# Two graph-attention layers: all source values made before the targets, adjacency masks transposed as pairs of bytes, and equal blocks of 1024 targets

## The chip, the core and the metric

The kernel runs on one core of one Trainium2 chip. The metric is the device time of one execution in microseconds (us). Before the change it is 3523.2 us, the median of three runs (3519.84 to 3524.52). The profiled execution has a span of 3524.0 us.

The engines are named as in the profile: PE is TensorE (PEld its weight loads), DVE is VectorE, ACT is ScalarE, POOL is GpSimd, SP is SyncE, whose queue issues the DMA transfers.

## What is computed

Three layers over 4096 nodes with 256 features, with one adjacency matrix `adj` (4096 x 4096, int32): two graph-attention layers and one masked transformer layer.

```python
def _gat_layer(x, adj_mat, W, a):              # 8 heads of O = 32
    Wh = einsum('nd,hdo->hno', x, W)
    src = einsum('hno,ho->hn', Wh, a[:, :O])
    dst = einsum('hno,ho->hn', Wh, a[:, O:])
    e = leaky_relu(src[:, :, None] + dst[:, None, :], 0.2)
    e = where(adj_mat[None] > 0, e, NEG_INF)
    alpha = softmax(e, axis=-1)
    return transpose(einsum('hnm,hmo->hno', alpha, Wh), (1, 0, 2)).reshape(N, -1)

h   = elu(_gat_layer(x, adj, W1, a1)) + x
out = elu(_gat_layer(h, adj, W2, a2)) + h
# then: layer norm, q/k/v, masked softmax attention, projection, feed-forward with gelu
```

The exponential of a leaky ReLU of a sum is one of two products of a factor of the target and a factor of the source; which one holds is a comparison of `src` with `-dst`. So a graph layer needs no exponential per pair: for each pair of nodes and each head it needs one bit, `src >= -dst` and `adj > 0`. These bits are made as bytes that TensorE reads as fp8, and the sums over the sources are matrix products of those bytes with tables of "values" (`vst`) of the sources. A last set of products with the mask alone gives the sum over all neighbours.

## The kernel before

A layer is a list of groups. A group is one block of targets, one pair of heads `p` and 512 sources `g` (four tiles `m` of 128). With eight target tiles it has 8 x 4 x 4 = 128 matmuls. "Chunk" stands below for 512 sources as they are prepared, `q` in the code.

```python
TILES = ((4, 4, 8, 8, 8), (8, 8, 8, 8))        # target tiles of 128, per layer and block

def mask_turn(w, k, t, r):                     # a unit of mask work: 128 targets, 1024 sources
    v = rows_p.tile([P, MC, P], BF, name="adj_bf", bufs=2)
    nc.vector.tensor_scalar(v..., r, 1.0, -(2.0**-30), op0=ALU.min, op1=ALU.max)   # the clip
    pt = turn_bank([P, MC, P], BF)             # two PSUM banks for all of this
    for m in range(MC):                        # MC = 8
        nc.tensor.transpose(pt[:, m, :], v[:, m, :], ident)
    nc.scalar.activation(staged[0]..., pt, AF.Identity, saturate=False)            # the eviction
    ...                                        # written to DRAM when 512 targets are done

def values(l, q, t):                           # the values of one tile of 128 sources
    pv = turn_bank([P, 512], F32)
    ...                                        # 2 matmuls, each issued as two passes
    nc.vector.tensor_scalar(L.negd[:, at, :], pv[...], -1.0, None, op0=ALU.mult)
    nc.scalar.activation(L.r[:, at, :], pv[...], AF.Exp, scale=LRELU - 1.0)        # g_r
    nc.vector.tensor_reduce(L.tops[...], pv[:, :D], AX.X, ALU.max, ...)            # g_tops
    for i in range(2):
        nc.scalar.activation(big[:, i, :], L.negd[:, at, :], AF.Exp, ...)
        nc.vector.tensor_scalar(prod[:, :, i, O], big[:, i, :], UP, None, op0=ALU.mult)
    nc.vector.tensor_tensor(prod[...], pv..., prod..., op=ALU.mult)                # the product
    nc.scalar.copy(halves[:, :, 0, :], part)                                       # the cast
    nc.vector.tensor_tensor(halves[:, :, 1, :], part, halves[:, :, 0, :], op=ALU.subtract)

def compare(l, nb, p, g, s_b):                 # the bytes of one group
    for i in range(G):                         # G = 4
        for j in range(2):
            if j == 1 or mt % MC == MC - 1:
                nc.scalar.activation(to.bitcast(I8), s, AF.Sign, bias=negd, scale=-1.0)   # L1021
            else:
                nc.vector.tensor_scalar(to, s, negd, None, op0=ALU.is_ge, saturate=False) # L1023
    nc.vector.tensor_tensor(both, both, mask..., op=ALU.bitwise_and)                      # L1026
```

At the start of a layer chunks 0 to 2 are prepared (`features`: transposes of the rows and two ACT copies; `term_rows`: a matmul, a copy and a store; four times `values`), then the groups begin, and chunks 3 to 7 are prepared in slots between the matmuls of the first groups. The comparisons of a group are made two groups ahead. After the last group of a pair of heads, `pair_end` works out its result on DVE and ACT in four steps that run beside later groups. The order on each engine is left to the scheduler of the programming framework.

The transformer follows: normalised rows and their q, k and v by matmuls (lines 1419 and 1440), the halves of q and k through DRAM into stacked tiles `u_k` and `u_q`, attention (lines 1480 to 1580) and projection with feed-forward (lines 1628 to 1676). There the first queries and masks are loaded after the last q/k/v block:

```python
        for nb in range(NNB):                  # q, k, v of 512 rows
            ...
            if i == 1:
                stack(k_st[:, :, cols], 1, (0, 0, 1, 1), cols)
        ...
        load_queries(0)
        for k in range(NT // MC):
            load_chunk(0, k)
        # attention follows, in an order fixed by the program
```

Of the kernel before, what the change touches and what calls it, by code (L numbers as in the profile page):

```python
# [14 lines left out]
U8 = mybir.dt.uint8  # L15
AF = mybir.ActivationFunctionType
# [5 lines left out]
P = 128  # L22
# [698 lines left out]
TILES = ((4, 4, 8, 8, 8), (8, 8, 8, 8))  # L721
# [27 lines left out]
def graph_attention(  # L749
# [32 lines left out]
    MC = 8  # L782
    G = 4
    NG = NT // G
# [9 lines left out]
    mask_p = ctx.enter_context(tc.tile_pool(name="g_mask", bufs=11))  # L794
    stage_p = ctx.enter_context(tc.tile_pool(name="g_stage", bufs=2))
    rows_p = ctx.enter_context(tc.tile_pool(name="g_rows", bufs=3))
# [8 lines left out]
    make_identity(nc, ident_f)  # L805

    vst = [keep.tile([P, G, H, 2 * VW], F16, name=f"vst{q}") for q in range(NG)]

    def turn_bank(shape, dtype):
        return ps.tile(shape, dtype, name="turn", tag="turn", bufs=2)  # L810

# [8 lines left out]
    nc.vector.tensor_scalar(checks.column(), pt[:, 0:1], 2.0**-20, None, op0=ALU.is_equal)  # L820


    masks = {}

    def mask_loads(w, k, t):

        r = rows_p.tile([P, MC * P], I32, name="g_rows")
        at = w * HB + t * P
        nc.sync.dma_start(r, adj[at : at + P, k * MC * P : (k + 1) * MC * P])
        return r  # L830

    staged = {}

    def mask_turn(w, k, t, r):

        if t == 0:
            if w == 0:
                staged[0] = mask_p.tile([P, 2, G, HB], F8, name="mask")
                views = [staged[0][:, i : i + 1] for i in range(2)]
                masks.setdefault((0, 0), []).extend(views)  # L840
            else:
                staged[0] = stage_p.tile([P, 2, G, HB], F8, name="stage")
        v = rows_p.tile([P, MC, P], BF, name="adj_bf", bufs=2)
        nc.vector.tensor_scalar(
            v.rearrange("p m s -> p (m s)"), r, 1.0, -(2.0**-30), op0=ALU.min, op1=ALU.max
        )
        pt = turn_bank([P, MC, P], BF)
        for m in range(MC):
            nc.tensor.transpose(pt[:, m, :], v[:, m, :], ident)  # L849
        nc.scalar.activation(  # L850
            staged[0].rearrange("p i g n -> p (i g) n")[:, :, t * P : (t + 1) * P],
            pt,
            AF.Identity,
            saturate=False,
        )
        if t == HB // P - 1:
            nc.sync.dma_start(
                mask_d[w][2 * k : 2 * k + 2].rearrange("c p n -> p c n"),
                staged[0].rearrange("p i g n -> p i (g n)").bitcast(U8),
            )  # L860

    def mask_fetch(l, nb, c):
        b = mask_p.tile([P, NW, G, HB], F8, name="mask")
        first = STARTS[l][nb] * P // HB
        n = TILES[l][nb] * P // HB
        for i in range(n):
            nc.sync.dma_start(
                b[:, i].rearrange("p g n -> p (g n)").bitcast(U8), mask_d[first + i][c]
            )
        masks.setdefault((l, nb), []).append(b[:, :n])  # L870
# [6 lines left out]
    for l, (w, a) in enumerate(weights):  # L877
        L = Layer()
        L.w_ext = keep.tile([P, DC, D + 2 * H], F32, name=f"g_w_ext{l}")
# [27 lines left out]
    def features(l, q):  # L907
# [5 lines left out]
        for c in range(DC):  # L913
            pt = turn_bank([P, HB], F32)
# [6 lines left out]
    def term_rows(l, q):  # L921

        L = layers[l]
        pr = turn_bank([P, HB], F32)
# [12 lines left out]
    def values(l, q, t):  # L937

        L = layers[l]
        pv = turn_bank([P, 512], F32)  # L940
# [31 lines left out]
        nc.vector.tensor_tensor(halves[:, :, 1, :], part, halves[:, :, 0, :], op=ALU.subtract)  # L972
# [9 lines left out]

    def preparation(l, q):

        steps = [lambda: (term_rows(l, q), values(l, q, 0))]
        steps += [lambda t=t: values(l, q, t) for t in range(1, G)]
        if q + 1 < NG:
            steps.insert(0, lambda: features(l, q + 1))
        else:
            steps.append(lambda: check_values(l))  # L990
        return steps
# [16 lines left out]
    def compare(l, nb, p, g, s_b):  # L1008

        L = layers[l]  # L1010
        nw = TILES[l][nb] * P // HB
        t8 = t_p.tile([P, 2, NW, G, HB], F8, name="t8")
        for i in range(G):
            mt = g * G + i
            for j in range(2):
                to = t8[:, j, :nw, i, :]
                s = s_b[:, j, : nw * HB].rearrange("p (w n) -> p w n", n=HB)
                negd = L.negd[:, mt, 2 * p + j : 2 * p + j + 1]

                if j == 1 or mt % MC == MC - 1:  # L1020
# [3 lines left out]
        both = t8[:, :, :nw].rearrange("p j w g n -> p j (w g n)").bitcast(I32)  # L1024
        mask = masks[l, nb][g].rearrange("p w g n -> p (w g n)").bitcast(I32)
        nc.vector.tensor_tensor(  # L1026
            both, both, mask.unsqueeze(1).to_broadcast(list(both.shape)), op=ALU.bitwise_and
        )
        return t8

    def pair_end(l, nb, p, ev):
# [37 lines left out]
        def step_divide():  # L1069
# [4 lines left out]
            z = block("e_z", O)  # L1074
            nc.vector.tensor_tensor(
                z, y[:, :, :, :O], inv.unsqueeze(3).to_broadcast([P, n, 2, O]), op=ALU.mult
# [5 lines left out]
        def step_out():  # L1082

            z, ex, x = (held[k].rearrange("p t j o -> p (t j o)") for k in ("z", "ex", "x"))
# [19 lines left out]

    turns = {}
    for nb in range(1, len(TILES[0])):
        first, n = STARTS[0][nb] * P // HB, TILES[0][nb] * P // HB
        units = [
            (first + i, k, t) for k in range(NT // MC) for i in range(n) for t in range(HB // P)
        ]  # L1110
        since, until = (NG, 3 * NG) if nb == 1 else (0, 3 * NG + 3)
        for u, unit in enumerate(units):
            at = (nb - 1) * per_block + since + u * (until - since) // len(units)
            turns.setdefault(at, []).append(unit)
    ordered = [u for i in sorted(turns) for u in turns[i]]
    loaded = {}
    AHEAD = 2

    def load_turns(n):

        while ordered and n > 0:
            u = ordered.pop(0)
            loaded[u] = mask_loads(*u)
            n -= 1
# [9 lines left out]
    def beside(i):  # L1134
# [5 lines left out]
        for u in turns.get(i, ()):  # L1140
            mask_turn(*u, loaded.pop(u))
            load_turns(1)
        if p + 1 == H // 2 and following(l, nb):
            for c in ((0, 1, 2), (), (), (3,), (4,), (5,), (6,), (7,))[g]:
                mask_fetch(*following(l, nb), c)

    def prepare(i):

        if i < len(groups):
            l, nb, p, g = groups[i]  # L1150
            s8[i] = compare(l, nb, p, g, s_of[l, nb, p])

    slots = []
    per = HB // P
    first_units = [(0, k, t) for k in range(NT // MC) for t in range(per)]
    ev = acc = None
    for i, (l, nb, p, g) in enumerate(groups):
        start = nb == 0 and p == 0
        if start and g == 0:

            features(l, 0)
            for q in range(2):
                for step in preparation(l, q):
                    step()
            while l > 0 and later:
                take()
            if l == 0:
                own = [mask_loads(*u) for u in first_units[:AHEAD]]
                for j in range(per):
# [591 lines left out]
```

## Time and profile before

| stage | from, us | to, us |
|---|---|---|
| graph layer 0 | 0 | 961 |
| graph layer 1 | 961 | 1783 |
| q, k, v | 1783 | 1893 |
| attention, with its start | 1893 | 3224 |
| projection and feed-forward | 3224 | 3524 |

The stages are read from the timeline: the last matmul of line 1234 of a layer, and the first and last of the lines named above.

| group of instructions | count | mean, ns |
|---|---|---|
| compare on ACT, 1024 targets (L1021) | 1008 | 1159 (1065 of busy time each, as they overlap) |
| compare on DVE, 1024 targets (L1023) | 784 | 746 (688 of busy time each) |
| AND with the mask, 2048 int32 (L1026) | 224 | 2288 |
| the same for half blocks, 1024 int32 | 64 | 1221 |
| clip (L844) | 128 | 685 |
| mask eviction (L850) | 128 | about 1035 |
| subtraction of `values` (L972) | 64 | 700 |

A window line of the profile gives the stretch, its length, then for PE, PEld, DVE, ACT and POOL the busy time with the number of instructions in brackets, then the granted TensorE clock (1.00 is full), the DMA share and GB/s. Restricted to one source line, it has only the engines of that line. A line of the list of groups gives line, engine, operation, output and inputs, shapes and count, then busy us and mean ns, then the idle time of the engine just before these instructions and what ended it. Of the 40 slices, each stands for 88 us, and a digit is the busy share in tenths.

### The profile page before, as it was taken

To read this page: it belongs to the slowest core of one execution; us is meant where nothing else is said; L and a number is where in the kernel's file an instruction comes from. 1 tells how busy PE (TensorE), PEld (TensorE's weight loads), DVE (VectorE), ACT (ScalarE), POOL (GpSimd) and SP (SyncE) were. 2 spreads that over 40 slices of the span, in tenths; PEclk is the share of its full clock that TensorE was granted. 3 is DMA by queue.
4 is the path that set the end of the run, shared out by engine and by line. 5 is a ranking of instruction groups with operands and counts; after the bars stand their busy time and mean duration, and the time that the engine had idled before them with its cause. 6 is when DMAs were issued, how large, how long until landed. Compare 5 with 4: busy or idle time off the path is not lost.

```text
span 3524.0 us, 99099 instructions
## 1 busy us (share of the span) xinstructions
PE 3357.4 (95%) x43715; PEld 2128.8 (60%) x43715; DVE 2903.2 (82%) x3580; ACT 2730.9 (77%) x3528; POOL 1239.1 (35%) x538
## 2 busy tenths in 40 slices
PE   6898999999989999999987999999999999997998
PEld 4698999999969999999963111111111121112666
DVE  5898999999889999999944999999999999996111
ACT  4799999998778888888854777777777777775332
POOL 0000000000000000000001999999999999996110
PEclk8999999999999999999998999999999999998999
DMA  4357554441221312111156010101010110002110
GB/s 140 123 191 242 167 167 157 157 123 39 68 62 33 86 39 80 45 58 37 26 135 171 10 40 13 37 19 31 25 25 25 25 37 13 28 9 68 44 47 25
DMA packets 199560, 252.76 MB, mean 72 GB/s; under 512 B 88080, under 2 KB 134672, under 8 KB 199120
## 3 DMA queue, kind: packets, MB, share of 16 engines
q1 hardware_dynamic: 199120, 246.34, 23.3%
q8 instruction: 344, 5.64, 0.7%
q14 instruction: 96, 0.79, 0.1%
HBM read 203.83 MB, written 42.47 MB: 70 GB/s over the span
## 4 chain that ended last, share of the span: by engine, by line
PE 73%; DVE 11%; ACT 9%; DMA 3%; issue 2%; POOL 2%; SPq 0%; DVEq 0%; ACTq 0%; POOLq 0%
PE bank L1234 34%; PE u_ps L1480 12%; PE u_av L1494 11%; PE u_dn L1494 6%; ACT t L1021 5%; DVE u_e L1489 4%; PE misc L1666 3%; PE misc L1419 2%; POOL u_both L1580 2%; DVE t L1023 1%; ACT u_ps L1487 1%; ACT stage L850 1%; DVE t L1026 1%; PE misc L1650 1%; PE turn L926 1%
## 5 line engine op out<-in xcount | busy, mean ns | idle before, releaser
L1234 PE MATMUL bank<-vst,t 128*128 128x66 f16 (+1 forms) x24576 | 1517.9, 203 | 22.0 <-DVE t L1026 15.5
L1234 PEld LDWEIGHTS <-t 128*128 128x128 fp8e4 x24576 | 1505.6, 97 | 33.2 <-DVE t L1026 18.0
L1234 PE MATMUL bank<-vst,mask 128*128 128x132 f16 x8192 | 1503.5, 222 | 0.0
L1021 ACT ACTIVATE t<-s_b,g_negd 128x1024 int8<-128x1024 f32 (+1 forms) x1296 | 1260.0, 1063 | 88.8 <-PE bank L1234 88.1
L1489 DVE SCALAR_TENSOR_TENSOR u_e<-u_mask,u_ps 128x1024 f32<-128x1024 uint8 x1024 | 1201.7, 1215 | 100.7 <-ACT u_ps L1487 95.8
L1580 POOL TENSOR_TENSOR u_both<-u_e 128x1024 f32<-128x1024 f32 x512 | 1199.8, 2367 | 238.5 <-DVE u_e L1489 238.3
L1487 ACT ACTIVATE u_ps<-u_ps 128x1024 f32<-128x1024 f32 x1024 | 1010.8, 1008 | 296.2 <-PE u_ps L1480 277.2
L1234 PEld LDWEIGHTS <-mask 128*128 128x128 fp8e4 x8192 | 803.6, 98 | 1.9 <-issue 0.9
L1026 DVE TENSOR_TENSOR t<-t,mask 128x2048 int32<-128x2048 int32 (+1 forms) x288 | 590.6, 2051 | 119.5 <-ACT t L1021 109.8
L1023 DVE TENSOR_SCALAR t<-s_b,g_negd 128x1024 fp8e4<-128x1024 f32 (+1 forms) x1008 | 638.5, 687 | 2.7 <-PE bank L1234 2.3
masks.py:197 POOL MEMSET u_ident<- 128x128 f32 x1 | 0.2, 204 | 1785.7 <-DMA u_wq<-in_L_gnn_w_qkv_dram 1785.7
L1480 PE MATMUL u_ps<-u_q,u_k 128*128 128x512 f16 x2048 | 580.5, 384 | 36.8 <-DMA u_q<-half_d 21.7
L1480 PEld LDWEIGHTS <-u_k 128*128 128x128 f16 x2048 | 139.2, 97 | 743.7 <-issue 685.4
L1494 PE MATMUL u_av<-u_e,u_v 128*32 128x512 f32 x4096 | 547.1, 605 | 0.0
L1494 PE MATMUL u_dn<-u_both,u_ones 128*32 128x512 f32 x2048 | 274.0, 605 | 1.3 <-POOL u_both L1580 1.3
L1494 PEld LDWEIGHTS u_av<-u_e,u_v 128*32 128x32 f32 x4096 | 80.9, 108 | 219.1 <-issue 211.3
L1657 ACT ACTIVATE u_hid<-misc,u_b 128x512 f32<-128x512 f32 x64 | 42.3, 683 | 142.9 <-PE misc L1650 142.8
L850 ACT ACTIVATE stage<-turn 128x1024 fp8e4<-128x1024 bf16 x112 | 114.2, 1037 | 1.1 <-PE turn L849 1.0
L1673 DVE TENSOR_TENSOR u_xres<-u_xres,misc 128x256 f32<-128x256 f32 x32 | 13.5, 421 | 122.7 <-PE misc L1666 122.7
L1666 PE MATMUL misc<-u_w,u_hid 128*128 128x256 f32 x512 | 111.8, 379 | 0.0
L1650 PE MATMUL misc<-ln_cols,u_w 128*128 128x512 f32 x256 | 111.2, 592 | 0.0
L1494 PEld LDWEIGHTS u_dn<-u_both,u_ones 128*32 128x32 f32 x2048 | 40.6, 108 | 110.9 <-issue 108.4
(104 smaller groups left out, 1749.8 us busy)
## 6 DMA issues: line engine op xcount, KB each, us to landing
g_rows<-in_adj_dram SPq DMA_DIRECT2D x128, 512.0 KB
mask<-mask SPq DMA_DIRECT2D x120, 256.0 KB
s_b<-s_d SPq DMA_DIRECT2D x56, 512.0 KB
u_mask<-mask SPq DMA_DIRECT2D x32, 512.0 KB
mask<-stage SPq DMA_DIRECT2D x28, 512.0 KB
half_d<-u_halves SPq DMA_DIRECT2D x32, 256.0 KB
u_k<-half_d SPq DMA_DIRECT2D x32, 256.0 KB
u_q<-half_d SPq DMA_DIRECT2D x32, 256.0 KB
```

The lines of the kernel that those rows point to most:

```text
L850: nc.scalar.activation(staged[0].rearrange("p i g n -> p (i g) n")[:, :, t * P : (t + 1) * P], pt, AF.Identity, saturate=False,)
L1021: nc.scalar.activation(to.bitcast(I8), s, AF.Sign, bias=negd, scale=-1.0)
L1023: nc.vector.tensor_scalar(to, s, negd, None, op0=ALU.is_ge, saturate=False)
L1026: nc.vector.tensor_tensor(both, both, mask.unsqueeze(1).to_broadcast(list(both.shape)), op=ALU.bitwise_and)
L1234: nc.tensor.matmul(to, left, right, start=k not in opened, stop=last)
L1480: nc.tensor.matmul(ps[:, j, :], k_st[:, h, mt * P : (mt + 1) * P], q_st[:, h, :], start=True, stop=True,)
L1487: nc.scalar.activation(ps, ps, AF.Exp, scale=SCALE)
L1489: nc.vector.scalar_tensor_tensor(e, mask, 0.0, ps, op0=ALU.not_equal, op1=ALU.mult)
L1494: nc.tensor.matmul(to[j * O : (j + 1) * O, :], lefts[j], es[j // 2][:, j % 2, :], start=start, stop=stop,)
L1580: nc.gpsimd.tensor_tensor(both, es_of[i - 1][u], es_of[i][u], op=ALU.add)
L1650: nc.tensor.matmul(ph, w1_sb[:, k, f * P : (f + 1) * P], hn[:, k, :], start=(k == 0), stop=(k == DC - 1),)
L1666: nc.tensor.matmul(po[:, :D], hid[:, f, at : at + P], w2_sb[:, f, :], start=(f == 0), stop=(f == FC - 1),)
```

## The change

It restructures the two graph layers and moves some loads of the transformer. Its parts:

- **Blocks.** Layer 0 gets four blocks of 1024 targets, as layer 1 has.
- **Masks as pairs of bytes.** A unit of mask work now loads 256 targets by 512 sources, target pairs side by side in a partition. The clip writes one byte (fp8) per element, the two targets of a pair next to each other; the pair is read as one 16-bit number, so that one transpose of 128 x 128 two-byte elements moves 256 targets. The eviction copies 16-bit numbers. The number of units stays 128.
- **All values first.** At the start of each layer `begin` prepares all eight chunks before the first group. For layer 0 the mask units of the first five source chunks of block 0 are made in between, and the comparisons of the first two groups are placed in chunks 5 and 6. The preparation uses the six accumulator banks, which are free then, in place of the two "turn" banks.
- **Subtraction on POOL.** The last step of `values` moves from DVE to POOL.
- **Order.** The order of PE, ACT and DVE in the graph layers is that of the program: comparisons, mask steps and `pair_end` steps are spread between the matmuls of a group.
- **Transformer.** Key stacks are read back one block later, the first queries and mask chunks are loaded during q, k and v, some pools change size and place, and the projection's weights are loaded first.

```diff
-TILES = ((4, 4, 8, 8, 8), (8, 8, 8, 8))
+TILES = ((8, 8, 8, 8), (8, 8, 8, 8))
...
+    def mask_load(nb, c, i):
+        r = rows_p.tile([P, 2, G * P], I32, name="g_adj", bufs=3)
+        ...  # adj[at : at + 2 * P, ...].rearrange("(k r) m -> k r m", r=2)
+    def mask_clip(nb, c, i):
+        v = rows_p.tile([P, G * P, 2], F8, name="adj_8", bufs=4)
+        nc.vector.tensor_scalar(v.rearrange("p m r -> p r m"), loaded.pop((nb, c, i)),
+            1.0, -(2.0**-30), op0=ALU.min, op1=ALU.max, saturate=False)
+        clipped[nb, c, i] = v.rearrange("p m r -> p (m r)").bitcast(F16)
+        load_ahead(1)
+    def mask_turn(nb, c, i):
+        pt = turn_bank([P, G, P], F16)
+        for m in range(G):
+            nc.tensor.transpose(pt[:, m, :], v[:, m * P : (m + 1) * P], ident_h)
+        to = built[nb, c][:, i // 2].bitcast(U16)
+        nc.scalar.activation(to[...], pt.bitcast(U16), AF.Copy)
...
-        nc.vector.tensor_tensor(halves[:, :, 1, :], part, halves[:, :, 0, :], op=ALU.subtract)
+        nc.gpsimd.tensor_tensor(halves[:, :, 1, :], part, halves[:, :, 0, :], op=ALU.subtract)
...
+    def begin(l, first):
+        features(l, 0)
+        for q in range(NG):
+            if q + 1 < NG:
+                features(l, q + 1)
+            units = queue[...] if q >= 3 else []      # layer 0 only: four units a chunk
+            term_rows(l, q)
+            for t in range(G):
+                values(l, q, t)
+                if units:
+                    mask_clip(*units[t])
+                    if t > 0:
+                        mask_turn(*units[t - 1])
+            if units:
+                mask_turn(*units[-1])
+            take()                                    # a step of the last pair_end
+            if q in (5, 6):
+                for step in compare(first + q - 5):
+                    step()
...
+    ordered = {mybir.EngineType.PE, mybir.EngineType.Activation, mybir.EngineType.DVE}
+    ctx.enter_context(tc.manual_schedule(engines=ordered))
...
+            for step in side[len(side) * n // tiles : len(side) * (n + 1) // tiles]:
+                step()                                # mask steps, one pair_end step
+            if n % 2 == 0 or n == tiles - 1:
+                if ahead:
+                    ahead.pop(0)()                    # comparisons of group i + 2
...
+                for b in (nb - 1,) if nb + 1 < NNB else (nb - 1, nb):
+                    if b >= 0:
+                        stack(k_st[...], 1, (0, 0, 1, 1), at)
+                    if b == 0:
+                        load_queries(0)
+                if 2 <= nb < 2 + NT // MC:
+                    load_chunk(0, nb - 2)
```

After the start, the remaining mask units are spread evenly: units of the last three source chunks of block 0 fall on groups 0 to 2, four to each; those of block 1 on groups 8 to 27 (1.6 a group), those of blocks 2 and 3 on 28 groups each of the block before them (1.14 a group).

## The prediction

> **What bounds the kernel now.** The page comes first: its engine totals, then its slices, because one total hides stages with different limits.
>
> ```profile
> PE 3357.4 (95%) x43715; PEld 2128.8 (60%) x43715; DVE 2903.2 (82%) x3580; ACT 2730.9 (77%) x3528; POOL 1239.1 (35%) x538
> ...
> PE   6898999999989999999987999999999999997998
> DVE  5898999999889999999944999999999999996111
> ACT  4799999998778888888854777777777777775332
> ```
>
> TensorE is busy nearly everywhere, but "busy" is not "at its rate". So I cut the span where the slices change and counted only the graph matmuls (line 1234) in each stretch: time and matmuls, (x...) being the count.
>
> ```profile
> 0.00:160.00 160.00, 35.74 (x612) 33.80 (x613) 0.89 0.42 131
> 160.00:216.00 56.00, 44.58 (x929) 42.96 (x927) 1.00 0.70 225
> 216.00:350.00 134.00, 110.10 (x2228) 107.42 (x2228) 0.96 0.63 202
> 350.00:434.00 84.00, 75.58 (x1617) 74.08 (x1614) 1.00 0.53 175
> 434.00:740.00 306.00, 287.65 (x6165) 283.56 (x6166) 1.00 0.50 157
> 740.00:961.00 221.00, 221.00 (x4844) 220.54 (x4841) 1.00 0.22 64
> 961.00:1067.00 106.00, 36.33 (x713) 34.50 (x709) 0.97 0.21 62
> 1067.00:1783.00 716.00, 715.58 (x15669) 713.95 (x15670) 1.00 0.17 50
> ```
>
> In the clean stretches the chain of waits runs 1024 matmuls in 46.67 us, 45.6 ns each, so a layer's 16384 need 747 us and a group of 128 needs 5.83 us. Layer 0 takes 961 us (214 above its floor, 189 of them before 434 us), layer 1 takes 822 (75 above). All engines' busy time in the first stretches says why:
>
> ```profile
> 216.00:350.00 134.00, 122.18 (x2474) 119.70 (x2474) 122.72 (x248) 132.11 (x221) 0.00 (x0) 0.96 0.63 202
> 350.00:434.00 84.00, 80.47 (x1722) 79.35 (x1720) 78.32 (x109) 82.94 (x104) 0.00 (x0) 1.00 0.53 175
> 434.00:740.00 306.00, 305.04 (x6573) 303.61 (x6574) 283.60 (x345) 293.60 (x347) 0.00 (x0) 1.00 0.50 157
> ```
>
> The fourth busy figure is ScalarE: 132 of 134 and 83 of 84 us. It bounds the first blocks. From 434 on PE bounds, paying for 408 transposes as well. The last piece is the seams, where PE idles: from the list of groups,
>
> ```profile
> L1480 PE MATMUL u_ps<-u_q,u_k 128*128 128x512 f16 x2048 | 580.5, 384 | 36.8 <-DMA u_q<-half_d 21.7
> ```
>
> a single 21.7 us wait before attention; the timeline also has PE without QKV matmuls from 1783 to 1803.
>
> **What the Trainium skill says.** "VectorE: DVE Perf Modes", section "The perf-mode tier table", gives fp32 `tensor_scalar` in SBUF two elements a cycle and fp32 `tensor_tensor` one. The trace agrees: a compare over 1024 columns takes 690 ns back to back, the mask AND over 2048 int32 takes 2288. The same page ("What auto-detection actually checks") makes the two-port mode depend on one source, SBUF and even outer dimensions, not on type or stride. So I take the new clip (int32 in, one byte out at a stride of two) at the old clip's rate; no run here shows that form. "Advanced Engine Details and Errata", section "Mode Summary", says that GpSimd and two-port Vector instructions share a port and block each other. POOL is 0.00 busy throughout the graph stage, so this trace is silent, and the change puts POOL work just there.
>
> **The change, part by part.**
>
> *Equal blocks.* Two half blocks (64 groups) become one full block (32 groups). DVE: 224 compares of 98.8 us and 64 ANDs of 78.0 become 32 x (3.5 x 0.688 + 2.288) = 150: 27 less. ACT: 288 compares of 186.3 become 144 x 1.065 = 153: 33 less.
>
> *Pairs of bytes.* 128 units of eight transposes become 128 of four. In 434 to 740 a transpose costs (306 - 6165 x 0.0456)/408 = 61 ns of PE, so 512 fewer save 31 us. Evictions: 128 x 1031 ns become 128 of 512 columns, taken like the 587 ns copy of `g_ft`, so 55 us less ACT. The clip keeps 1024 elements: 88 us, unchanged if the mode holds.
>
> *Subtract to POOL.* 64 x 700 ns = 45 us leave DVE. POOL does 1024 f32 in 2.37 us, hence an estimated 1.2 us each, hidden.
>
> *All values first.* This costs. Before, five of eight chunks of values ran beside graph matmuls; now none does, in either layer. In the fixed order one tile is a chain: product (0.69), ACT cast (0.63), the next tile's `g_r` (0.18), `g_tops` (0.42, which in the trace waits for `g_r`), two scalings (0.24). That is 2.16, less three overlaps of 0.08 and plus small hand-overs: 2.1 us a tile. A chunk is 4 x 2.1 plus the ACT copies of features and term rows (1.6) = 10.0 us. PE's own work is about 8 (transposes 1.5, term rows 1.9, values 4 x 1.18), no bound.
>
> Layer 0's start: first values at 23.6 as now; first chunk 8.4, two more 20. The five chunks that carry mask units cost more: clip and eviction lengthen a tile to 2.6, and PE must wait for the last clip before it does the next chunk's transposes, term rows and first value (0.7 + 5.1 us, then ACT and DVE work), so product to product across chunks is about 7.7. That gives 12.2 + 4 x 15.5 = 74. Two early compares with their ANDs: 7. Sum 133, so graph matmuls start near 134.
>
> Groups after it: a full group costs DVE 5.28 us (646.5 us / 15669 matmuls x 128), ACT 5.13, PE 5.83. Groups 0 to 2 carry four mask units each: DVE 5.3 + 4 x 0.69 = 8. Block 0 then has 20 groups with 1.6 units (DVE 6.4, PE 6.2), blocks 1 and 2 have 28 each with 1.14 (PE 5.83 + 1.14 x 4 x 0.061 = 6.11, DVE 6.05), the remaining 49 run at 5.83. Layer 0: 134 + 24 + 128 + 56 x 6.13 (343) + 49 x 5.83 (286) = **915, 46 less than 961**. That leaves nothing for in-order losses in the clean groups; the queues may run up to two groups ahead of PE there, and I hold that to be enough.
>
> Layer 1's start: about 7 us to the first value, 8.4 + 7 x 10 = 78, the last pair's ending in the same queues 7, two compares with ANDs 11: 103. With 747 this is **850, 28 more than 822**.
>
> *Seams.* In the changed order the load of `u_wq` stands at the start of layer 1, not behind its end, and the first `u_x` follow early: QKV can begin about 12 us after the last graph matmul instead of 20.5, because six squares, a square-root table load and the transposes still follow the last evacuation: -8. The first queries, keys and masks are loaded during QKV: of the 21.7 us wait I count 18 as gained, since the last casts and the Exp table load remain. The projection's weights first: -4, as PE waited 11.9 us there for data.
>
> Sum: -46 + 28 - 8 - 18 - 4 = -48, or **3475 us**. Attention's 1298 us and the feed-forward are untouched.
>
> **Rivals.**
> 1. *The clip falls to one element a cycle.* The interleaved one-byte writes from two ports fall in the same word; nothing in the profile speaks for or against it. 1.22 us, what the AND over 1024 columns takes in this trace, would put DVE at 5.28 + 1.14 x 1.22 = 6.7 in masked groups and 7.2 in block 0: some +55 us, giving 3530. About one chance in four.
> 2. *The fixed order wins or loses.* For a win: all values being ready lets the first eight groups run clean, and six PSUM banks instead of two serve the preparation. For a loss: today's order overlaps two tiles of values (four tiles in about 7.3 us at 982 to 989, subtraction included), and stretches with 100% PE leave nothing to gain. If chunks with masks take 12 rather than 15.5, 3460; if all the starts serialize further, 3515.
> 3. *POOL blocks the two-port compares and clips* in the starts: 20 clips and 14 compares, up to 1.2 us each, would be +15 to +30.
> 4. *The seams were hidden anyway.* Attention may wait for late key blocks instead of queries; then 18 of the gain go. The first key blocks are loaded well before, so I give it little.
>
> **Range and chances.** The largest independent terms are the two starts (each about +-15), the clip (0 to +55) and the seams (+-10). They give 3425 to 3540 around 3478, the centre moved up a little for rival 1. Faster by 2% means under 3452.7, which needs shorter starts and no rival: 0.26. Slower by 2% means 3593.7, which needs rivals 1 and 3 and more: 0.05.
>
> **What would show it.** First clean run of graph matmuls near 134 us, and layer 0's end near 915; a gap without graph matmuls of about 100 us at layer 1's start, then 46.67 us per 1024; layer 1 longer by about 28; clip mean near 690 ns, the mask eviction near 590; layer 0's masked groups at about 6.1 us; no `u_q` wait over 5 us; attention steady in the same 1298. The prediction is wrong if the clip is far from 690 ns, if chunks of values take far from 10 us, or if layer 0's masked groups leave PE idle.

## The result, and the profile after

The changed kernel takes **3569.6 us** (median of 4 runs, 3566.1 to 3571.7) against 3523.9 us for the kernel before (3519.8 to 3525.3): a ratio of **1.013, 95% interval 1.011 to 1.015**. I had said 3478, with 3425 to 3540 as the range. It is 92 us above that centre and 95 above the sum of the parts (3475).

The first lines of the page after, to be laid beside those of before:

```profile
PE 3355.5 (94%) x43204; PEld 2117.5 (59%) x43204; DVE 2895.6 (81%) x3329; ACT 2659.0 (75%) x3382; POOL 1314.4 (37%) x602
...
PE   6799999999959999999988999999999999997999
...
DVE  4789988989768999999963999999999999996111
ACT  3688888888747889888874777777777777775322
```

ScalarE has lost 72 us of busy time (2731 to 2659), where I had counted on 88. VectorE has lost only 8 of the 72 that I had counted on. Summed by instruction it lost 45: the subtract is gone (-45), compares and ANDs fell by 24, but the 128 scalings of the values, which had 166 ns each before, have 357 now (+24). The other 37 lie in the counting: the profile counts overlapping instructions once, and they overlap less now. The 5 in PE's twelfth slice (8 before) is the start of layer 1. No engine is full over the graph layers, and yet the time grew. So I cut the span again and counted graph matmuls alone (line 1261 now; columns: stretch, its length, PE time and matmuls, weight loads, granted clock, DMA share, GB/s):

```profile
0.00:138.00 138.00, 0.00 (x0) 0.00 (x0) 0.80 0.51 151
138.00:752.00 614.00, 561.34 (x11709) 550.78 (x11710) 0.98 0.53 165
752.00:966.00 214.00, 213.86 (x4671) 212.54 (x4668) 1.00 0.20 61
966.00:1072.00 106.00, 0.53 (x12) 0.38 (x9) 0.84 0.20 61
1072.00:1832.00 760.00, 754.92 (x16384) 749.49 (x16384) 0.99 0.17 50
```

Row 3 runs at 45.8 ns a matmul, the same clean rate as before. Row 2, the groups that carry mask units, takes 614 us where 11709 matmuls at 45.7 ns and 432 transposes at 61 ns need 561. The same stretch with all engines (PE, PEld, DVE, ACT, POOL busy):

```profile
138.00:752.00 614.00, 574.46 (x12141) 569.60 (x12142) 551.34 (x671) 526.43 (x661) 1.15 (x1) 0.98 0.53 165
```

574, 551 and 526 of 614 us: **nobody is the bound there**. That is the mark of engines waiting for each other.

From these views each run can be cut in four: the start of layer 0 (to the first graph matmul), the graph stretch of layer 0, the gap without graph matmuls, the graph stretch of layer 1. All in us, in steps of 0.5, of the profiled run; the last column is the ratio of the timed runs to the kernel before.

| kernel | start 0 | groups 0 | gap | groups 1 | time | ratio (95%) |
|---|---|---|---|---|---|---|
| before | interleaved | to 961.5 | interleaved | to 1784 | 3524 | 1 |
| after | 138 | 829 | 105.5 | 759.5 | 3569.6 | 1.013 (1.011-1.015) |
| no_fixed_order | 86.5 | 788.5 | 66 | 751 | 3428.1 | 0.973 (0.971-0.974) |
| starts_free | 98.5 | 828.5 | 72 | 756.5 | 3489.8 | 0.991 (0.989-0.992) |
| clip_two_ahead | 135.5 | 808.5 | 105.5 | 759.5 | 3547.7 | 1.007 (1.006-1.009) |
| clip_and_compares_early | 138 | 799.5 | 105.5 | 755.5 | 3539.4 | 1.005 (1.003-1.006) |
| start_staggered | 138 | 827.5 | 106 | 757 | 3567.5 | 1.013 (1.011-1.014) |
| cast_two_behind | 130 | 828 | 82 | 754.5 | 3533.5 | 1.003 (1.002-1.004) |
| fixed_order_mended | 114.5 | 800.5 | 81 | 750.5 | 3486.5 | 0.990 (0.989-0.992) |
| subtract_on_vector | 161.5 | 828.5 | 113.5 | 761.5 | 3601.9 | 1.022 (1.021-1.024) |
| no_fixed_order_vector_sub | 79 | 796.5 | 57 | 760 | 3429.0 | 0.973 (0.971-0.975) |

### The profile page after: what moved, and what is told of

Read it like the earlier page. It is cut to its first block, busy times and chain, and to the rows that moved or that the text cites. A ratio compares the mean times of both kernels' runs of the same rounds, so it can differ in the third digit from the quotient of the medians.

```text
span 3567.7 us, 97732 instructions
## 1 busy us (share of the span) xinstructions
PE 3355.5 (94%) x43204; PEld 2117.5 (59%) x43204; DVE 2895.6 (81%) x3329; ACT 2659.0 (75%) x3382; POOL 1314.4 (37%) x602
## 4 chain that ended last, share of the span: by engine, by line
PE 68%; DVE 10%; ACT 6%; POOL 2%; DMA 2%; issue 1%; SPq 0%; ACTq 0%; DVEq 0%; POOLq 0%
PE bank L1261 32%; PE u_ps L1516 12%; PE u_av L1530 11%; PE u_dn L1530 6%; DVE u_e L1525 4%; PE misc L1699 3%; ACT t L1045 2%; PE misc L1464 2%; POOL u_both L1613 1%; ACT u_ps L1523 1%; DVE t L1052 1%; PE misc L1483 1%; PE misc L1683 1%; ACT ln_square L1368 1%; DVE t L1047 1%
## 5 line engine op out<-in xcount | busy, mean ns | idle before, releaser
L1045 ACT ACTIVATE t<-s_b,g_negd 128x1024 int8<-128x1024 f32 x1152 | 1236.0, 1163 | 32.6 <-PE bank L1261 32.6
L1052 DVE TENSOR_TENSOR t<-t,mask 128x2048 int32<-128x2048 int32 x256 | 586.1, 2289 | 145.6 <-ACT t L1045 135.9
L1047 DVE TENSOR_SCALAR t<-s_b,g_negd 128x1024 fp8e4<-128x1024 f32 x896 | 621.9, 751 | 0.0
L1005 POOL TENSOR_TENSOR vst<-g_prod,vst 128x528 f16<-128x528 f32 x64 | 75.4, 1178 | 1005.9 <-ACT g_r L986 929.8
L885 PE MATMUL turn<-g_ident_h,adj 128*128 128x128 f16 x512 | 53.9, 232 | 70.2 <-DVE adj L863 40.7
L1004 ACT CAST vst<-g_prod 128x528 f16<-128x528 f32 x64 | 40.5, 632 | 102.1 <-DVE g_prod L996 56.7
```

What stands on the lines that cost most here:

```text
L1005: nc.gpsimd.tensor_tensor(halves[:, :, 1, :], part, halves[:, :, 0, :], op=ALU.subtract)
L1052: nc.vector.tensor_tensor(both, both, m32.unsqueeze(1).to_broadcast(list(both.shape)), op=ALU.bitwise_and)
```

## Experiment 1: is it the fixed order?

Theory A: the change's work is as cheap as predicted, and the fixed order of PE, ScalarE and VectorE loses more than it saves. Two runs test it, one takes the order away and one mends a single place in it.

```diff
-    ctx.enter_context(tc.manual_schedule(engines=ordered))   # graph layers
```

> The changed kernel, with the graph layers' engine order left to the framework again (the one line that fixes it is taken out), all else as changed. Theory A: the fixed order costs the masked groups of layer 0 some 43 us, because PE's mask transposes stand behind a clip that DVE reaches late after every end of a pair. Then the order alone gives this back: the stretch from the first graph matmul (138 us) to the last masked group takes about 570 us and not 614, the dips every 53 us are gone, and the total falls to about 3525. Theory B: the masked groups lack DVE or ScalarE time in any order; then the stretch stays within 10 us of 614 and the total within 10 us of 3570. Theory C: the framework's order is worse than the fixed one (values that wait, accumulators held); then over 3590.

Measured: **3428.1 us**, ratio 0.973. One line is worth 141 us. The changed kernel without it beats both. That is three times the 45 that I expected of it: not only layer 0's groups (829 to 788.5), but the start (138 to 86.5), the gap (105.5 to 66) and layer 1's groups (759.5 to 751) got shorter: -51.5 - 40.5 - 39.5 - 8.5 = -140. Theory B falls: the masked groups did not stay within 10 us of 614.

The same cuts of this kernel, graph matmuls alone (line 1259 there), and then its masked groups with all engines:

```profile
86.00:660.00 574.00, 551.42 (x11666) 539.21 (x11667) 1.00 0.56 177
...
875.00:941.00 66.00, 0.00 (x0) 0.10 (x1) 0.97 0.33 98
941.00:1692.00 751.00, 746.07 (x16384) 745.24 (x16383) 1.00 0.18 51
```

```profile
86.00:660.00 574.00, 561.88 (x12113) 558.33 (x12113) 554.43 (x700) 521.77 (x682) 8.93 (x8) 1.00 0.56 177
```

About as many masked groups (11666 graph matmuls for 11709) now take 574 us in place of 614. The fifth busy figure, POOL's, shows one thing more: eight subtracts fall into this stretch, one in the kernel after. The free order starts the groups while the last values are still being made. Its last product comes at 100.4 us, 14 after its first graph matmul; in the kernel after the last product comes at 136.6, before the first graph matmul. So of the 51.5 us of the start, 36 are a faster preparation and the rest is preparation that now runs beside the first groups.

## Experiment 2: where the groups lose, clips behind late work

The timeline of the kernel after, around the end of a pair (start, duration, engine, line, output<-inputs; in brackets the idle time before and who ended it):

```profile
424.57 1.25 DVE L1080 TENSOR_TENSOR ev_broad<-ev_broad 128x1056 f32<-128x1056 f32 x1
...
427.76 0.43 DVE L1093 TENSOR_TENSOR e_y<-e_y,ev_narrow 128x264 f32<-128x264 f32 x1
428.10 0.69 DVE L863 TENSOR_SCALAR adj<-g_adj 128x1024 fp8e4<-128x1024 int32 x1
428.70 2.28 DVE L1052 TENSOR_TENSOR t<-t,mask 128x2048 int32<-128x2048 int32 x1
428.85 0.40 PE L885 MATMUL turn<-g_ident_h,adj 128*128 128x128 f16 x4 [2.17 <-DVE adj L863]
429.29 0.60 ACT L887 ACTIVATE stage<-turn 128x512 uint16<-128x512 uint16 x1 [2.24 <-PE turn L885]
```

VectorE is late after the compares and spends 3.5 us on the pair's sums before it comes to a clip of 0.69. PE has graph matmuls ready, but in its queue the four transposes come first, so it stands for 2.2 us; ScalarE stands too, behind the eviction, and so its next compares are late. The Trainium skill says in "PSUM — Partial Sum Buffer", section "Engine vs sequencer instructions", that the queues of ScalarE, VectorE and GpSimd are strictly first in, first out, and that matmuls start and complete in program order; the trace agrees, with no matmul of PE in these 2.2 us. Between 200 and 740 us these waits are (us in total, times, longest):

```profile
DVE t L1052 <- ACT t L1045: 44.9, 31, 3.8
ACT stage L887 <- PE turn L885: 38.2, 31, 2.5
PEld L885 <- DVE adj L863: 34.6, 22, 3.0
PE turn L885 <- DVE adj L863: 31.2, 21, 2.9
```

(The two PE rows are the same idle time, seen by the weight load and by the matmul.) In the free order, from 200 to 640 us, the clip holds PE once, and the ANDs wait 6.6 us in 440 in place of 44.9 in 540:

```profile
DVE t L1052 <- ACT t L1045: 6.6, 9, 1.0
...
PEld L885 <- DVE adj L863: 0.6, 1, 0.6
```

First mend: the clip is emitted two groups ahead of its transposes.

```diff
-            for u in turns.get(i + 1, ()):
+            for u in turns.get(i + 2, ()):
                 side.append(lambda u=u: mask_clip(*u))
```

> The changed kernel, with the clip of each mask unit emitted two groups ahead of its transposes instead of one; nothing else. Theory A (PE's transposes stand behind a clip that DVE reaches late after the end of a pair): most of the 43 us lost in layer 0's masked groups come back, the dips of PE every 53 us flatten, total about 3532. Theory B (DVE has no time left in the groups with a pair's end: 4.7 of compares and AND, 0.7 of clip and 3.5 of sums, 8.9 us against 6.1): the stall only moves, total within 10 us of 3570.

Measured: 3547.7, 22 us better, layer 0's groups 829 to 808.5. Half of the 40.5 us that the free order gains there. The theory's direction holds, its size (38) does not; the other half is elsewhere. In this run PE waits for the ANDs, and they for ScalarE's compares. In the fixed order those stand between the evacuations of a pair's last group, each of which waits for PE's tile. Second mend, on top:

```diff
+            while ahead:            # in the last group of a pair: compares and AND
+                ahead.pop(0)()      # before the first evacuation
...
-            if n % 2 == 0 or n == tiles - 1:
+            if g < NG - 1 and (n % 2 == 0 or n == tiles - 1):
```

> The changed kernel with its fixed order, the clips two groups ahead (that alone gave 22 us: layer 0's groups 808.5 in place of 829, free order 788), and in the last group of a pair the compares and the AND of the group two ahead ahead of the evacuations, in place of between them. Theory C (ScalarE's compares are tied to PE's pace by the evacuations in the fixed order, and so VectorE's AND comes late): the rest of the loss comes back, layer 0's groups fall to about 792, layer 1's from 759.5 to 752, total about 3525. Theory D (the loss left is in VectorE's sums in the order): total within 6 us of the 3548 of the clips alone. Rival E: evacuations come too late for the next pair's accumulators, and each of the 32 ends of a pair waits: over 3555.

Measured: 3539.4, another 8 us: layer 0's groups 799.5, layer 1's 755.5. Between C (3525) and D (3548); C accounts for a little under half of what was left (9 us of the 20 in layer 0, 4 of the 8.5 in layer 1). Rival E did not happen. The two mends take 29.5 of the 40.5 us in layer 0.

## Experiment 3: where the starts lose, a ring through two queues

> The changed kernel with the fixed order kept for the groups only: the two starts (values, first masks, first compares) are left to the framework's order. The run without any fixed order took 142 us off: first graph matmul about 90 in place of 138, the gap at layer 1's start 66 in place of 105.5, layer 0's groups 788 in place of 829, layer 1's 751 in place of 759.5. Theory A1 (the losses of the fixed order add up, start by start and group by group): this kernel gains the two starts, -45 and -40, and keeps the groups' 829 and 759.5: about 3485. Theory A2 (the framework hides the rest of a start beside the first groups, which a fixed order of the groups forbids): starts stay above 120 and 90, total over 3530.

```diff
-    ctx.enter_context(tc.manual_schedule(engines=ordered))
+    fixed = ExitStack()
...
+            fixed.close()
             begin(l, i)
+            fixed.enter_context(tc.manual_schedule(engines=ordered))
```

Measured: 3489.8; expected 3485. The starts gain 39.5 and 33.5 us, the groups keep their fixed 828.5 and nearly their 759.5 (756.5). A1 holds in the main, so starts and groups lose separately. The starts stay 12 and 6 us longer than in the free order, and that is A2 on a small scale: layer 0's last product comes at 99.0 us, with the first graph matmul at 98.7, so no preparation runs beside the first groups. Why the rest? In the kernel after, one turn from tile to tile in layer 1's start looks like this (from the timeline; ScalarE, VectorE and POOL):

```profile
1012.21 0.63 ACT L1004 CAST vst<-g_prod 128x528 f16<-128x528 f32 x1 [1.23 <-DVE g_negd L983]
1012.75 0.17 ACT L986 ACTIVATE g_r<-bank 128x8 f32<-128x8 f32 x1
...
1012.92 1.15 POOL L1005 TENSOR_TENSOR vst<-g_prod,vst 128x528 f16<-128x528 f32 x1 [3.28 <-ACT g_r L986]
1012.95 0.42 DVE L987 TENSOR_REDUCE g_tops<-bank 128x1 f32<-128x256 f32 x1 [0.76 <-ACT g_r L986]
1013.29 0.88 DVE L995 TENSOR_SCALAR g_prod<-g_big 128x8 f32<-128x8 f32 x2
1014.20 0.69 DVE L996 TENSOR_TENSOR g_prod<-bank,g_prod 128x512 f32<-128x512 f32 x1
...
1014.98 0.63 ACT L1004 CAST vst<-g_prod 128x528 f16<-128x528 f32 x1 [1.87 <-DVE g_negd L983]
```

From cast to cast 2.77 us, product to product as well: the ring of the prediction, with one member of the wrong size. The cast waits for the product, the next `g_r` stands behind the cast, `g_tops` waits for `g_r`, the scalings and the next product follow. The pair of scalings takes 0.88 and not 0.24, because POOL's subtract runs beside it. I first tried to break the ring by emitting a tile's products and cast after the next tile's `g_negd`, `g_r`, `g_tops` and exponentials (the order of emission, in short):

```diff
-    values(l, q, t)
+    terms(l, q, t + 1)       # matmuls, g_negd, g_r, g_tops, exponentials
+    products(l, q, t)        # scalings, product, cast, subtract
```

> The changed kernel with its fixed order, but each tile of values cut in two in the program: the products, casts and subtract of a tile are emitted behind the next tile's matmuls, g_negd, g_r, g_tops and two exponentials, so that ScalarE has the next g_r before it the cast that waits for the product. Theory A (a start loses its time to the chain product, cast, next g_r, next tops, scalings, product, in the order written): a tile takes about 1.8 us (DVE 0.16 + 0.42 + 2 x 0.36 + 0.69, or PE's 8 us a chunk) in place of some 2.7; layer 1's gap falls from 105.5 to about 80, layer 0's start from 138 to about 120, total about 3525. Theory B (the starts are held by the loads of x and of the masks, or by PE): under 8 us gained in all.

Measured: 3567.5, nothing. The gap is 106 us as before, and so Theory A seemed to fall. The timeline showed why: the ring had only been turned round. The cast of tile t still stood ahead of `g_r` of tile t+2, and `g_tops` of t+2 ahead of the scalings of t+1. Then the cast was moved a tile further back:

```diff
     terms(l, q, t + 1)
+    halved(q, t - 1)         # cast, subtract
     products(l, q, t)        # scalings, product
```

> The changed kernel with its fixed order, and the values cut in three in the program: g_negd, g_r, g_tops and the exponentials of tile t+1 first, then the cast and subtract of tile t-1, then the scalings and product of tile t. The stagger tried before left the cast of tile t in front of the next g_r on ScalarE, and that g_r in front of the scalings on VectorE, so product, cast, g_r, tops, scalings, product stayed one ring of 2.76 us a tile and nothing moved. Theory A (this ring is what a start loses): now the product is not in front of g_r any more; the ring is g_negd 0.16, wait 0.24, g_tops 0.42, scalings 0.24 to 0.88, product 0.69, 1.8 to 2.3 us a tile; layer 1's gap falls from 105.5 to 82 to 92, layer 0's start from 138 to 120 to 128; total 3535 to 3555. Theory B (loads, PE or POOL hold the starts): within 8 us of 3570.

Measured: **3533.5, 36 us better**; the gap falls to 82 us, layer 0's start to 130. Two casts of this run, 1.62 us apart:

```profile
1012.28 0.42 DVE L987 TENSOR_REDUCE g_tops<-bank 128x1 f32<-128x256 f32 x1 [0.24 <-ACT g_r L986]
1012.35 0.62 ACT L1011 CAST vst<-g_prod 128x528 f16<-128x528 f32 x1
1012.63 0.24 DVE L999 TENSOR_SCALAR g_prod<-g_big 128x8 f32<-128x8 f32 x2
1012.90 0.69 DVE L1000 TENSOR_TENSOR g_prod<-bank,g_prod 128x512 f32<-128x512 f32 x1
...
1013.97 0.62 ACT L1011 CAST vst<-g_prod 128x528 f16<-128x528 f32 x1
```

The scalings now end before the subtract begins, so they are back at 0.24 a pair. Layer 0's start gained less than expected (8 of 10 to 18), and the chunks with mask units show a reason: there the clips meet the subtract. From the same run:

```profile
82.35 1.14 POOL L1012 TENSOR_TENSOR vst<-g_prod,vst 128x528 f16<-128x528 f32 x1 [1.62 <-ACT vst L1011]
82.81 1.23 DVE L863 TENSOR_SCALAR adj<-g_adj 128x1024 fp8e4<-128x1024 int32 x1
...
84.10 0.61 PE L885 MATMUL turn<-g_ident_h,adj 128*128 128x128 f16 x4 [1.40 <-DVE adj L863]
```

A clip of 0.69 us takes 1.23 when it comes 0.46 after the subtract's start; 19 of the 20 clips of this start took over 1 us, none in the kernel after. At the end of a chunk PE's transposes also hold the next chunk's work. The last mend let the transposes of a chunk's last unit follow the next chunk's first value; with all the mends above it makes one kernel, still in a fixed order:

```diff
-            if units:
-                mask_turn(*units[-1])
+                if len(waiting) > (1 if units else 0):     # carried into the next chunk
+                    mask_turn(*waiting.pop(0))
```

> The changed kernel, still in its fixed order, with three mends of the program at once: the values in three pieces (alone -36), clips two groups ahead with the compares ahead of the evacuations (alone -30), and in layer 0's start the transposes of a chunk's last mask unit behind the next chunk's first value, so that PE does not wait for that clip. Theory A (the fixed order's loss of 141 us is made of such places, and they add): -36 - 30 and some -10 to -16 for the third, about 3490; layer 0's start 116 to 122, its groups 800, layer 1's gap 82, its groups 755. Theory F (most of the loss is not in these places but in the fixed order as such; the mends overlap): 3505 to 3540.

Measured: **3486.5** (expected 3490), ratio 0.990. That is 83 us off: 36 and 30 as the first two mends gave alone, and 17 left for the third, which was not run alone but shows where it was aimed, start 0 at 114.5 (130 without it). So Theory A holds as far as 83 of the 141 us. Of the other 58, 55 are the start (28), the gap (15) and layer 0's groups (12). About half of the start's 28 is the preparation that the free order makes beside the first groups (14 us, experiment 1): read from the traces, not tested by a run. For the rest no single place is shown.

> The same three mends with no fixed order in the graph layers, and the keys' and queries' loads on POOL's queue (3419 without the mends). Theory F1 (the framework plans its own order from what is ready, so the order in the program matters little there): within 8 us of 3419. Theory F2 (it follows the program where several instructions are ready, so the mends are worth a part there too): start 80, gap 60, total 3400 to 3411.

This takes the same mends, no fixed order, and the other queue of experiment 5. Measured: 3418.1, against 3419.5 without the mends. F1: where the framework orders the engines, the order in the program matters little.

## Experiment 4: POOL's subtract

```diff
-        nc.gpsimd.tensor_tensor(halves[:, :, 1, :], part, halves[:, :, 0, :], op=ALU.subtract)
+        nc.vector.tensor_tensor(halves[:, :, 1, :], part, halves[:, :, 0, :], op=ALU.subtract)
```

> The changed kernel, with the values' subtract (the low halves) back on VectorE, as before the change; nothing else. Theory P: the subtract on POOL blocks the two scalings (357 ns each now against 166 before) and so gains nothing: the scalings return to 166 ns, a tile of values takes 2.6 us either way, both starts stay within 5 us each of 138 and 115, total 3560 to 3580. Rival Q: the subtract on POOL is hidden and worth its 0.7 us of DVE a tile: then both starts grow by about 20 us each and the total is about 3610. Rival R: POOL costs more than it takes off: starts shorter by 10 us each, total about 3550.

> The changed kernel without the fixed order in the graph layers, and with the values' subtract on VectorE. In the fixed order the subtract on VectorE cost 32 us, though the scalings went back from 357 to 167 ns. Theory Q (off DVE's queue it is worth its 0.7 us a tile also here, 64 tiles): about 3428 + 40 = 3465. Theory P (in a free order DVE's other work fills the waits, and the blocked scalings, 273 ns, and clips, 746 ns, give most of it back): 3428 to 3445.

Groups of the kernel after, then of the run with the subtract on VectorE (mean ns behind the comma):

```profile
L995 DVE TENSOR_SCALAR g_prod<-g_big 128x8 f32<-128x8 f32 x128 | 40.0, 357 | 0.2 <-issue 0.2
```

```profile
L995 DVE TENSOR_SCALAR g_prod<-g_big 128x8 f32<-128x8 f32 x128 | 15.2, 167 | 0.0
```

Last, one subtract on VectorE in the fixed order, and all 64 in the free order (idle time before them behind the last bar):

```profile
1025.12 0.71 DVE L1005 TENSOR_TENSOR vst<-g_prod,vst 128x528 f16<-128x528 f32 x1 [0.70 <-ACT vst L1004]
...
L1005 DVE TENSOR_TENSOR vst<-g_prod,vst 128x528 f16<-128x528 f32 x64 | 44.8, 701 | 2.9 <-ACT vst L1004 2.7
```

The blocking is real: without POOL's work the scalings take 167 ns. And yet the kernel got **slower**, 3601.9: Theory P was right about the scalings and wrong about the time. In the fixed order VectorE waits 0.7 us for the cast before it can subtract, and the clips of layer 0's start come later still (start 0 at 161.5). Rival Q is nearest in the total (3610), though the two starts grew by 23.5 and 8 and not by 20 each. In the free order the same edit gives 3429.0 against 3428.1, no difference: VectorE waits 2.7 us for all the casts together, not 0.7 for each. (The cuts of that run move, starts shorter and groups longer, since it begins the groups with 24 of 32 tiles of values made.) So in the fixed order the move to POOL is worth 32 us, and in the free order nothing. The Trainium skill, "SBUF — State Buffer", section "Who interferes with whom", says that GpSimd and a VectorE instruction in a two-port mode share a port pair, and that the one that issues second is blocked until the other ends. The clip above agrees: 0.46 + 1.23 = 1.69 us after the subtract's start, near the subtract's 1.14 plus a clip of 0.69 less some overlap.

## Experiment 5: the seams

The transformer part of the change alone, on the kernel before:

> The kernel before, with the changed transformer part alone (early queries, keys and masks, smaller pools in the QKV stage, projection weights first); graph layers as before. Theory S1: the seams are worth what the two profiles show of them together: about -7 from the first QKV matmul to the first attention matmul, +3 in the feed-forward, so 3517 to 3523, against the prediction's -30. Theory S2: the earlier queries are worth the predicted 18 us, and the changed graph layers' end took the rest; then about 3500. The QKV stage itself is expected to take some 107 us in place of 92 in either case, if its own pools or its loads lengthen it.

Measured: 3524.6, ratio 1.000 (0.999 to 1.001): S1 within a few us. The wait for `u_q` is gone: from the start of the last matmul of q and k to the first of attention is 4.5 us, 25.8 before. But from the first matmul of q and k to the last, called the QKV stage here, it now takes 108.5 us, 88.2 before. The later blocks all look like this (new seams on the kernel before):

```profile
1852.09 0.30 ACT L1345 ACTIVATE ln_dev<-ln_dev,u_eps 128x4 f32<-128x4 f32 x1
...
1852.71 1.38 DVE L1349 TENSOR_SCALAR ln_rows<-u_x,ln_mean,ln_dev 128x256 f32<-128x256 f32 x4
...
1853.17 2.19 PE L1365 MATMUL misc<-u_ident,ln_rows 128*128 128x128 f32 x8 [3.92 <-DVE ln_rows L1349]
```

The layer norm of a block comes just ahead of its own transposes, and PE stands for 3.9 us in each of four later blocks; in the kernel before PE waited for no norm once the stage was under way. I tested two causes in the free order, the number of its buffers and the queue:

```diff
-            ln = qkv.enter_context(tc.tile_pool(name="u_ln", bufs=2))
+            ln = qkv.enter_context(tc.tile_pool(name="u_ln", bufs=3))
```

> The changed kernel without the fixed order in the graph layers, and with three buffers in place of two for the layer norm's tiles of the QKV stage, as before the change. Theory L (with two buffers the norm of a block can only be written once the block two before it is transposed, which makes every block a chain and lengthens the stage from first to last QKV matmul from 88 to 103-108 us): 88 to 92 us again, and the total falls from 3428 to about 3412. Rival D (the added loads of keys, queries and masks delay the loads of x): the stage stays at 103, total 3428 within 4.

Measured: 3430.7, and the QKV stage takes 103 us as without it. Theory L falls.

```diff
         for a, kind in enumerate(order):          # stack(): keys and queries
-                nc.sync.dma_start(
+                nc.gpsimd.dma_start(
```

> The changed kernel without the fixed order in the graph layers, and with the loads of keys and queries issued by POOL's queue in place of SP's; three buffers for the layer norm did not shorten the QKV stage. Theory D (on SP's queue the loads of keys, which wait for stores, stand in front of the loads of x; the framework then plans each block's layer norm late, just ahead of its own transposes, and PE waits 3.9 us a block): the stage from first to last QKV matmul falls from 103 to 88 to 92 us with no later wait for queries, total 3428 to about 3413. Theory E (the order of the planned norms has another cause): within 4 us of 3428.

Measured: **3419.5**, ratio 0.971 (0.969 to 0.972); the QKV stage takes 92 us and the way to attention still 4.5. By the profile 11 us, in the timed runs 9 (3413 was expected). That is D in the main: with the loads of keys and queries on the queue that also loads `x`, the norms come late. That it is the framework's plan and not the transfer itself is argued, not shown; the trace with the new seams speaks for it, as VectorE takes the means of the last three blocks there right behind other work, with no wait for a load of `x`.

## Why the prediction was wrong, step by step

By the profile, the miss against the sum of the parts is 92 us (48 less was forecast, the span grew by 44): 51 in layer 0, 15 in layer 1 and 26 at the seams.

- **The sum for layer 0's masked groups** is the step that failed. It took the busiest engine's own time, 6.1 to 6.4 us a group (8 for the first three), as the time of the group, with no term for PE waiting in its order. For the 91.5 groups up to 752 us it gives 568; measured 614, and 574 without the fixed order. What it left out is the wait shown in experiment 2: the transposes, emitted between the matmuls of a group, stand in PE's queue behind a clip that VectorE reaches late, and ScalarE's compares behind them. The sign that the prediction named came true: "layer 0's masked groups leave PE idle". "I hold that to be enough", said of the clean groups, held in layer 0 (45.8 ns a matmul). From first to last graph matmul I had 781 us for layer 0; measured 829, and 788.5 without the fixed order, within 1% of the forecast.
- **The start of layer 0** came out at 138 (134 predicted), with one member of the wrong size. A plain chunk took 11.65 us, not 10.0, as a tile's ring is 2.72 to 2.77 and not 2.1 (the scalings 0.88, not 0.24); the chunks with masks and the two early compares took 80 (81 predicted). Rival 2 looked for the fixed order's loss in the starts ("if all the starts serialize further"). They came out near the forecast, and the loss lay in the groups. What the prediction did not see is that the start could be much shorter: 86.5 in the free order.
- **Layer 1** was predicted 28 longer and came out 42.5 longer: the gap at 105.5 (103), the groups at 759.5 (747). 8.5 of those 12.5 us go with the fixed order.
- **Clip and eviction** were right: 691 ns (690) and 594 to 620 (590). Rival 1 did not happen.
- **Rival 3** has the right mechanism, but it hit the scalings (191 ns on each of 128, 24 us) and not the clips, which kept 691 ns; and in the balance the move to POOL still gained 32 us.
- **Seams**: queries -18 was right as a wait, which fell by 21, but the QKV stage took 102.9 us in place of 88.2, which took back 15. I had looked at what ended the wait and not at what the earlier loads stood in front of. QKV began 16 us after the last graph matmul, as before (-8 predicted; the 20.5 that I started from was misread, its first matmul stands at 1800.3 and not at 1803). Projection and feed-forward took 300 us, 3 more (-4 predicted), but the same code took 294 to 303 in the other runs. Attention was untouched, as said (1313 us from its first matmul to its last, before and after).

What remains open: how the gain of the free order over the kernel before (96 us, of which 86 in layer 0) divides between equal blocks, byte pairs and values first. It was not tried.

## What to carry to other kernels

Before fixing an engine order, draw for each engine the instruction that stands at its head when another one is late: a short operation that feeds PE, put behind long work that nobody waits for, stops all three engines, though none is busy. Where one tile's last step and the next tile's first step share a queue, put more tiles between them, and follow the ring to its end; here one tile only turned the ring round and gained nothing, and a second broke it (36 us). A load brought forward is not free by itself: look at what it stands in front of; here another queue for it gave 9 us.

## What I had not expected of the hardware

Where PE waits, its own work takes longer too. The same stretch of the two kernels, all engines, the granted clock in the third column from the end, first after, then without the fixed order:

```profile
60.00:138.00 78.00, 49.85 (x185) 26.19 (x183) 51.79 (x123) 41.56 (x111) 21.98 (x19) 0.72 0.58 169
```

```profile
60.00:86.00 26.00, 20.45 (x99) 11.76 (x98) 24.32 (x59) 21.58 (x58) 12.33 (x9) 1.00 0.69 215
```

With PE busy 64% of the time the granted clock is 0.72, with 79% it is 1.00, and over both layers' values a matmul (128x272) takes 468 and 407 ns. It shows in the masked groups as well: nearly the same matmuls (12141 and 12113) keep PE busy for 574.5 us at a clock of 0.98 and for 561.9 at 1.00, so some 12 of the 40 us lost there look like PE's own work made longer (inferred from these means, not tested). The Trainium skill says in "TensorE: Matmul & The Clock Gate", section "What's actually happening", that the clock is held back by default and released by recent activity; these stretches agree. But the busy share alone does not set it: from 40 to 45 us PE was busy for 69% in both kernels, at a clock of 0.55 and of 1.00.
